# Second attention of a two-layer hybrid block: diagonal chunk mirrored through memory, row sums taken from the output

## The chip, the cores and the metric

The kernel runs on one core of a Trainium2 chip, all data in float32. The metric is device time in microseconds (us) of one launch; lower is better. The profile is of one further execution, recorded by the hardware profiler.

## The reference, cut to what matters

The input `x` is (8, 128, 48, 48): 8 samples, 128 channels, N = 2304 positions. Layer 0 is a group norm and a causal attention with a residual. Layer 1 works on tokens (one per position, 128 channels each):

```
t = tokens of x after layer 0                    # (8, 2304, 128)
h = ln(t)                                        # layer norm over the 128 channels, no gain, no bias
attn = softmax(h @ h^T)                          # "second attention": queries = keys = values = h
t = t + attn @ h
t = t + ffn(ln(t))                               # W, batch norm, then a recurrence over time
```

Two facts of the second attention are used below. The score matrix `h h^T` is symmetric, so the exponential of score (a, b) is also that of (b, a). And since `h` comes out of a layer norm with neither gain nor bias, its 128 channels add up to zero for every token, up to rounding.

## The kernel before, in words

Positions are cut into NB = 18 blocks of P = 128, and into NQ = 6 chunks of QC = 384 (QB = 3 blocks each). For each sample, class `Causal` runs the first attention and class `Full` the second, chunk of queries by chunk of queries. All work items of all samples stand in one list, `stream`; the main loop calls `begin` of item n (score matmul on TensorE, exponential on ScalarE) and `product` of item n - LAG, LAG = 3. So a probability tile is used three items after it was asked for. The first three items of the next sample's causal attention are slipped among the last six items of the second attention.

`Full` has two kinds of item. A **direct** item for key block m computes scores of that block against the 384 queries of chunk j (L1219), exponentiates them into `p` (L1221), and multiplies `p` with the token-major normed block `xhT` into the chunk's PSUM tile `o` (L1233). A direct item whose key chunk n lies behind the query chunk (n > j) is also kept for later: VectorE transposes it in 32 x 32 blocks into tile `t` (L1182), and once the three blocks of a chunk pair are in, `t` is stored to a DRAM tile `e` in one DMA (L1162). When the query chunk is n, the pair is loaded back into `g` by four DMAs, one for each 32 partitions (L1153), which completes the 128 x 128 transposition. A **turned** item then needs a product only (L1229). Chunk j has 3(6 - j) direct items, its own three blocks (the diagonal chunk) among them, and 3j turned ones. Pool `gpool` has three `g` buffers; `prefetch` loads up to three pairs ahead.

Row sums come from three places: ScalarE's accumulator output beside each exponential (`rows`), a VectorE reduction of each full `t` tile (`tsum`, L1190), and a matmul with the 0/1 matrix `same` (L1264) that adds the reduced pieces over partitions, masked by `mine`.

When a chunk is done, `after` copies `o` to SBUF and builds a chain of small steps (`sums`, `residual`, `rooted`, ...). Class `Stream` is a planner: it keeps a clock of its own, `now`, counted in TensorE time, and at every item `tick` emits up to two steps whose due time has come. `advance` and `finish` force steps of a chain out at once. The order of instructions on each engine is the order of emission. Nearly all DMAs are issued by SyncE (SP), in that order; an issue that has to wait holds up those behind it. Scratch tiles of chunk size have one or two buffers (`chunk_tile`), the causal attention's `ta` and `toc` one each. Products' PSUM pool `ps_o` has two buffers, `ps_t` for the chains has two, the pool of `p` six.

The causal attention treats its diagonal chunk by triangles already: item m = 3j + g computes only the columns from g*128 on, and GpSimd (POOL) masks the 128 x 128 block on the diagonal (L1023) before the product. Chain steps of a causal chunk end in `normed` (writes the token-major `xhT`) and `back` (transposes it, writes the channel-major `xh`).

Of the kernel before, what the change touches and what calls it, by code (L numbers as in the profile page):

```python
# [604 lines left out]
def fast_path(ctx: ExitStack, tc: tile.TileContext, x, pe, w_ffn, out, x_tok, w_qkv, w_pos, v_t, gamma_beta, flag):  # L605
    nc = tc.nc
# [60 lines left out]
    with ExitStack() as actx:  # L667
# [93 lines left out]
        for r in range(1 - R, R):  # L761
# [3 lines left out]
        mine = apool.tile([P, NQ - 1, R, QB], F32, tag="mine", name="mine")  # L765
        nc.gpsimd.memset(mine, 1.0)
        nc.gpsimd.affine_select(
            out=mine, in_=mine, compare_op=ALU.is_ge, fill=0.0, base=0, pattern=[[0, NQ - 1], [-SQ, R], [0, QB]], channel_multiplier=1
        )
        nc.gpsimd.affine_select(  # L770
            out=mine, in_=mine, compare_op=ALU.is_ge, fill=0.0, base=SQ - 1, pattern=[[0, NQ - 1], [SQ, R], [0, QB]], channel_multiplier=-1
# [217 lines left out]
        class Causal:  # L989
# [57 lines left out]
            def after(self, j, o):  # L1047
# [25 lines left out]
                def sums():  # L1073

                    tp = psum_t(f"dn_{b}_{j}")
                    k = R * QB
                    nc.tensor.matmul(tp[:, :k], same.rearrange("p a c -> p (a c)"), c["parts"], start=True, stop=True)  # L1077
                    own = small.tile([P, R, QB], F32, tag="ownc", name=f"ownc_{b}_{j}")
                    nc.vector.tensor_mul(own.rearrange("p a g -> p (a g)"), tp[:, :k], mine[:, 0].rearrange("p a g -> p (a g)"))
                    ri = small.tile([P, QB], F32, tag="ric", name=f"ric_{b}_{j}")  # L1080
                    nc.vector.tensor_reduce(ri, own.rearrange("p a g -> p g a"), AX.X, ALU.add)
                    nc.vector.reciprocal(ri, ri)
                    c["ri"] = ri
# [24 lines left out]
                def back():  # L1108
                    tp = transposed(c["y"], f"tb_{b}_{j}")
                    nc.scalar.copy(x_hat[b][1][:, cols], tp[:, :QC])  # L1110

                c["chain"] = normed_chunks[b, j] = st.add([
# [7 lines left out]
                    (back, 0.35, [("ACT", 0.5)]),  # L1120
                ], max(at, st.free["DVE"]) + 0.2 - st.now)

        class Full:
# [6 lines left out]
            def __init__(self, b):  # L1130
                self.b = b
                self.tsum, self.tiles, self.stored, self.loaded = {}, {}, {}, {}
                self.pairs = [(i, j) for j in range(NQ) for i in range(j)]
                self.used, self.to_store = 0, deque()

            @staticmethod
            def items():
                chunks = []
                for j in range(NQ):
                    behind = list(range(j + 1, NQ))  # L1140
                    ahead = [("direct", QB * n + g) for n in ([0] + behind if j == 0 else behind + [j]) for g in range(QB)]
                    turn = [("turned", i, g) for i in range(j) for g in range(QB)]
                    both = [((k + 0.5) / len(ahead), w) for k, w in enumerate(ahead)]
                    both += [((k + 0.5) / len(turn), w) for k, w in enumerate(turn)]
                    chunks.append([w for _, w in sorted(both, key=lambda e: e[0])])
                return listed(chunks)

            def load(self):
                i, j = self.pairs[len(self.loaded)]
                d, _ = self.stored[i, j]  # L1150
                g = gpool.tile([P, R, QB, QB, SQ], F32, tag="g", name=f"g_{self.b}_{i}_{j}")
                for r in range(R):
                    nc.sync.dma_start(  # L1153
                        g[ts(r, SQ)].rearrange("c a j m r -> c a (j m r)"),
                        d.rearrange("(a c) b f -> b c a f", a=R)[r],
                    )
                self.loaded[i, j] = g

            def store(self):
                j, n, t, at = self.to_store.popleft()  # L1160
                d = dpool.tile([P, R, QB * QB * SQ], F32, tag=f"e_{j}_{n}", name=f"e_{self.b}_{j}_{n}")
                nc.sync.dma_start(d, t.rearrange("p b j m r -> p b (j m r)"))  # L1162
                self.stored[j, n] = d, max(at, st.now)

            def prefetch(self):
                while self.to_store and self.to_store[0][3] <= st.now:
                    self.store()
                n = len(self.loaded)
                if n < len(self.pairs) and n < self.used + 3 and self.pairs[n] in self.stored:
                    if self.stored[self.pairs[n]][1] + 6.0 <= st.now:  # L1170
                        self.load()

            def turned(self, j, m, p, ready):
# [12 lines left out]
                if g == QB - 1:  # L1186
                    self.to_store.append((j, n, t, at))
                    if j not in self.tsum:
                        self.tsum[j] = small2.tile([P, NQ - 1, R * QB], F32, tag="tsum", name=f"tsum_{b}_{j}")
                    nc.vector.tensor_reduce(  # L1190
                        self.tsum[j][:, n - j - 1, :], t.rearrange("p b j m r -> p (b j) (m r)"), AX.X, ALU.add
                    )
                    st.then(at, [("DVE", 1.35)])
                    del self.tiles[n]

            def begin(self, j, what, first):
                b = self.b
                if first and j == 0:
                    self.rows = small2.tile([P, NB, NQ], F32, tag="rows", name=f"rows_{b}")
# [9 lines left out]
                if what[0] == "turned":  # L1209
# [5 lines left out]
                    return self.loaded[i, j][:, :, g, :, :].rearrange("p a m r -> p m a r"), 0.0  # L1215
                m = what[1]
                xh = x_hat[b][1]
                s = psum_s(f"s1_{b}_{j}_{m}")
                nc.tensor.matmul(s[:, :QC], xh[:, ts(m, P)], xh[:, ts(j, QC)], start=True, stop=True)  # L1219
                p = pp.tile([P, QC], F32, tag="p", name=f"p1_{b}_{j}_{m}")  # L1220
                nc.scalar.activation(p, s[:, :QC], AF.Exp, bias=shift, accum_out=self.rows[:, m, j : j + 1])  # L1221
                return p, st.then(st.spend(QC * US), [("ACT", 0.58)])

            def product(self, j, what, o, p, ready, first, last):
                xhT = x_hat[self.b][0]
                if what[0] == "turned":
# [3 lines left out]
                    if g == QB - 1:  # L1230
                        self.used += 1
                else:
                    nc.tensor.matmul(o[:, :QC], xhT[:, what[1], :], p, start=first, stop=last)  # L1233
                    st.then(ready, [("ACT", 0.2)])
                    if what[1] // QB > j:
                        self.turned(j, what[1], p, ready)
                st.spend(QC * US, ready)

            def after(self, j, o):
                b, rows, tsum = self.b, self.rows, self.tsum  # L1240
# [4 lines left out]
                if far:  # L1245
                    ot = turn_result(o, f"f_{b}_{j}", c, True)
                    at = st.then(st.now, [("DVE", 0.57)])
                    through = token_major(c, ot, f"f_{b}_{j}", "tof", 4)
                else:
                    o_sb = chunk_tile("o", f"of_{b}_{j}", c, 2)  # L1250
# [5 lines left out]
                def sums():  # L1256

                    dn = small2.tile([P, QB], F32, tag="dn", name=f"dn_{b}_{j}")
                    nc.vector.tensor_reduce(dn, rows[:, QB * j : QB * (j + 1), : j + 1], AX.X, ALU.add)
                    n = NQ - 1 - j  # L1260
                    if n:
                        tp = psum_t(f"ts_{b}_{j}")
                        k = n * R * QB
                        nc.tensor.matmul(  # L1264
                            tp[:, :k], same.rearrange("p a c -> p (a c)"), tsum[j][:, :n, :].rearrange("p n k -> p (n k)"),
                            start=True, stop=True,
                        )
                        own = small2.tile([P, NQ - 1, R, QB], F32, tag="own", name=f"own_{b}_{j}")
                        nc.vector.tensor_mul(
                            own[:, :n].rearrange("p n a g -> p (n a g)"), tp[:, :k], mine[:, :n].rearrange("p n a g -> p (n a g)")  # L1270
                        )
                        more = small2.tile([P, QB], F32, tag="more", name=f"more_{b}_{j}")
                        nc.vector.tensor_reduce(more, own[:, :n].rearrange("p n a g -> p g (n a)"), AX.X, ALU.add)
                        nc.vector.tensor_add(dn, dn, more)
                    ri = small.tile([P, QB], F32, tag="ri", name=f"ri_{b}_{j}")
                    nc.vector.reciprocal(ri, dn)
                    c["ri"] = ri

                def residual():
                    tp = None if far else transposed(o_sb, f"of_t_{b}_{j}")  # L1280
                    t2 = chunk_tile("t2", f"t2_{b}_{j}", c, 5 if last else 2 + F, bufs=1)
# [9 lines left out]
                    if not last:  # L1291
                        c["tt"] = chunk_tile("turn", f"tt_{b}_{j}", c, 5 + F, bufs=1)
# [22 lines left out]
                def fetch():  # L1315
                    c["t2x"] = chunk_tile("t2x", f"t2x_{b}_{j}", c, 7 + F, bufs=1)
                    nc.sync.dma_start(c["t2x"], t2_d[:, b, cols])
                    c["scale"] = chunk_tile("scale", f"scale_{b}_{j}", c, 8 + F, bufs=1)
# [14 lines left out]
                def normed():  # L1333
                    c["x2"] = chunk_tile("t2x", f"x2_{b}_{j}", c, 6, bufs=1)
# [4 lines left out]
                def keep(t2x):  # L1339

                    k = j % (SG // SJ)
                    if before is not None:
                        st.advance(before, 7 if k else len(before.steps) + before.done)
# [14 lines left out]
                def back():  # L1358
                    tp = turned_back(c["x2"], f"tx_{b}_{j}")
                    c["xc"] = chunk_tile("scale", f"xc_{b}_{j}", c, 7, bufs=1)  # L1360
# [21 lines left out]
                else:  # L1382
# [9 lines left out]
                    (sums, 0.15, [("DVE", 0.8)]),  # L1392
                    (residual, 0.0 if far else 0.35, [("DVE", 3.2)]),
# [243 lines left out]
```

## Time and profile before

| what | value |
|---|---|
| median of 3 runs | 1771.99 us (1771.1 to 1772.96) |
| profiled execution, its own time | 1769.93 us |
| its span, first to last instruction | 1768.1 us |
| mean granted TensorE clock | 0.993 |
| busy: PE / DVE / ACT / POOL | 1739.9 / 1299.7 / 762.5 / 194.9 us |
| instructions | 22177 |
| moved by DMA | 262.00 MB |

PE is TensorE's matmuls, PEld its weight loads (they overlap), DVE is VectorE, ACT is ScalarE, POOL is GpSimd, SP is SyncE. A float32 matmul shows as two PE records, so 504 matmuls read x1008. A PE record's duration runs from its start to its end and overlaps the next record's: the price of a matmul is the distance between starts, not the mean in the row. From one sample's start to the next the profile repeats every 207.65 us (a sample's same three-product group starts at 645.10 and at 852.76 us); a last stage of some 65 us is the recurrence.

### The profile page before, as it was taken

How to read it: one execution, taken by the hardware profiler on the slowest of the kernel's cores; microseconds unless marked ns; L12 is line 12 of the kernel's file. 1: busy time of each engine (PE TensorE's matmuls, PEld its weight loads, DVE VectorE, ACT ScalarE, POOL GpSimd, SP SyncE). 2: the span in 40 equal slices, each digit the busy share in tenths (PEclk: the TensorE clock that was granted, in tenths of full speed). 3: DMA queues.
4: the chain of work that ended last, by engine and by line, in shares of the span. 5: the costliest groups of instructions: out<-in, count | busy, mean ns of one | idle time of the engine just before them, and what ended most of it. 6: DMA issues, size and time to landing. Idle time of an engine off the chain costs nothing.

```text
span 1768.1 us, 22177 instructions
## 1 busy us (share of the span) xinstructions
PE 1739.9 (98%) x6215; PEld 1092.2 (62%) x6215; DVE 1299.7 (74%) x3355; ACT 762.5 (43%) x1836; POOL 194.9 (11%) x301
## 2 busy tenths in 40 slices
PE   9999999999999999999999999999999999999996
PEld 5666566665666566665666656665666656666565
DVE  4868668876887668786687767876687866877467
ACT  2344434443345434444344443454344543444445
POOL 1110011100110001100111001200011001110006
PEclk8999999999999999999999999999999999999998
DMA  3405672257533584156731575334832468116768
GB/s 141 139 23 182 184 203 93 89 184 193 146 103 121 157 235 130 47 167 183 209 99 68 190 197 157 107 108 157 228 120 77 148 183 217 56 46 199 194 231 217
DMA packets 206056, 262.00 MB, mean 148 GB/s; under 512 B 90113, under 2 KB 175010, under 8 KB 205412
## 3 DMA queue, kind: packets, MB, share of 16 engines
q1 hardware_dynamic: 204972, 257.47, 48.2%
q0 software_dynamic: 720, 2.62, 1.0%
q8 instruction: 52, 0.85, 0.2%
q14 instruction: 80, 0.66, 0.1%
q10 hardware_dynamic: 232, 0.40, 0.1%
HBM read 150.24 MB, written 110.17 MB: 147 GB/s over the span
## 4 chain that ended last, share of the span: by engine, by line
PE 96%; DMA 1%; DVE 1%; ACT 1%; issue 0%; SPq 0%; POOL 0%; ACTq 0%; DVEq 0%; POOLq 0%
PE o L1233 19%; PE s L1219 19%; PE s L1018 17%; PE o L1029 17%; PE o L1229 13%; PE pj L879 4%; PE pj L882 2%; PE z L1550 2%; PE wx L1325 2%; PE of_t L939 1%; PE tb L939 1%; PE pb L837 0%; DMA x<-in_x_dram 0%; PE dn L1077 0%; PE ts L1264 0%
## 5 line engine op out<-in xcount | busy, mean ns | idle before, releaser
L1221 ACT ACTIVATE p<-s,shift 128x384 f32<-128x384 f32 x504 | 292.3, 580 | 479.1 <-PE s L1219 464.5
L1020 ACT ACTIVATE p<-s 128x384 f32<-128x384 f32 (+2 forms) x504 | 231.6, 460 | 426.0 <-PE s L1018 372.1
L1219 PE MATMUL s<-xh 128*128 128x384 f32 x1008 | 410.6, 489 | 0.0
L1233 PE MATMUL o<-p,xhT 128*128 128x384 f32 x1008 | 404.2, 488 | 5.8 <-ACT p L1221 5.8
L1018 PE MATMUL s<-q,k 128*128 128x384 f32 (+2 forms) x1008 | 382.1, 461 | 0.1
L1029 PE MATMUL o<-p,vT 128*128 128x384 f32 (+2 forms) x1008 | 377.6, 457 | 0.0
L1229 PE MATMUL o<-g,xhT 128*128 128x384 f32 x720 | 281.3, 489 | 0.5 <-issue 0.5
L1233 PEld LDWEIGHTS o<-p,xhT 128*128 128x128 f32 x1008 | 189.4, 190 | 133.2 <-ACT p L1221 10.3
L1029 PEld LDWEIGHTS o<-p,vT 128*128 128x128 f32 x1008 | 189.2, 191 | 114.3 <-issue 0.6
L1219 PEld LDWEIGHTS s<-xh 128*128 128x128 f32 x1008 | 186.7, 191 | 114.8
L1018 PEld LDWEIGHTS s<-q,k 128*128 128x128 f32 x1008 | 183.2, 191 | 96.9 <-issue 0.9
L1044 DVE TENSOR_TENSOR acc<-acc,p 128x384 f32<-128x384 f32 (+2 forms) x408 | 208.9, 512 | 33.0 <-POOL p L1023 8.7
L1182 DVE STREAM_TRANSPOSE t<-p 128x384 f32<-128x384 f32 x360 | 187.2, 550 | 37.6 <-ACT p L1221 35.9
L1229 PEld LDWEIGHTS o<-g,xhT 128*128 128x128 f32 x720 | 133.6, 191 | 82.5 <-DMA g<-e 0.7
L1190 DVE TENSOR_REDUCE tsum<-t 128x12 f32<-128x1152 f32 x120 | 162.4, 1353 | 4.2
L884 DVE TENSOR_TENSOR z<-pj,pb 128x384 f32<-128x384 f32 x144 | 78.9, 548 | 109.3 <-PE pj L879 92.7
L1023 POOL TENSOR_TENSOR p<-p,triu 128x128 f32<-128x128 f32 x144 | 72.5, 505 | 607.4 <-ACT p L1020 476.5
L1299 POOL TENSOR_TENSOR roots<-ve_f,mhalf 128x3 f32<-128x3 f32 x48 | 40.8, 849 | 520.6 <-DVE ve_f L923 520.6
L1221 ACT ACTIVATION_READ_ACCUMULATOR p<-s,shift 128x1 f32 x504 | 97.2, 193 | 0.0
L879 PE MATMUL pj<-xn,wT 128*128 128x384 f32 x192 | 79.9, 501 | 1.4 <-DVE xn L872 1.4
L929 POOL TENSOR_TENSOR rs_c<-ve_c,mhalf 128x3 f32<-128x3 f32 x48 | 45.4, 947 | 215.6 <-DVE ve_c L923 215.6
L1326 DVE TENSOR_TENSOR scale<-wx,scale 128x384 f32<-128x384 f32 x46 | 25.4, 552 | 55.6 <-PE wx L1325 50.6
(242 smaller groups left out, 1471.0 us busy)
## 6 DMA issues: line engine op xcount, KB each, us to landing
e<-t SPq DMA_DIRECT2D x120, 576.0 KB
g<-e SPq DMA_DIRECT2D x480, 144.0 KB
pb<-posb_d SPq DMA_DIRECT2D x46, 576.0 KB
t1t<-in_x_tok_dram SPq DMA_DIRECT2D x48, 192.0 KB
t_d<-tt SPq DMA_DIRECT2D x184, 48.0 KB
t2x<-t_d SPq DMA_DIRECT2D x46, 192.0 KB
scale<-rs SPq DMA_DIRECT2D x46, 192.0 KB
x<-in_x_dram SPq DMA_DIRECT2D x14, 576.0 KB
```

Source lines behind the costliest of these rows:

```text
L879: nc.tensor.matmul(ps[:, :QC], wT[:, j, :], xn, start=True, stop=True)
L884: nc.vector.tensor_add(z, ps[:, :QC], c["pb"][:, j, :])
L1018: nc.tensor.matmul(s[:, off:QC], keys[b][:, ts(m, P)], queries[b, j][:, off:], start=True, stop=True)
L1020: nc.scalar.activation(p[:, off:], s[:, off:QC], AF.Exp, scale=SCALE)
L1029: nc.tensor.matmul(o[:, off:QC], vals[b][:, ts(m, P)], p[:, off:], start=first, stop=last)
L1044: nc.vector.tensor_add(a[:, off:], a[:, off:], p[:, off:])
L1182: nc.vector.transpose(t[:, :, :, g, :].rearrange("p b j r -> p j b r"), p.rearrange("p (j b r) -> p j b r", j=QB, b=R))
L1190: nc.vector.tensor_reduce(self.tsum[j][:, n - j - 1, :], t.rearrange("p b j m r -> p (b j) (m r)"), AX.X, ALU.add)
L1219: nc.tensor.matmul(s[:, :QC], xh[:, ts(m, P)], xh[:, ts(j, QC)], start=True, stop=True)
L1221: nc.scalar.activation(p, s[:, :QC], AF.Exp, bias=shift, accum_out=self.rows[:, m, j : j + 1])
L1229: nc.tensor.matmul(out_ap, xhT[:, QB * i + g, :], p, start=first, stop=last)
L1233: nc.tensor.matmul(o[:, :QC], xhT[:, what[1], :], p, start=first, stop=last)
```

## The change

1. **Mirror.** A direct item of the diagonal chunk (m = 3j + g) computes only the columns from g*128 on, for the score, the exponential and the product. The products left out come from transposes: blocks right of the diagonal of items g = 0 and g = 1 are transposed by VectorE in 32 x 32 blocks into `tm` (the tag of the causal `ta`), written to DRAM in one DMA, and read back by four DMAs into `gm` (the tag of the causal `to`). Two **mirrored** items per chunk, g = 1 (128 columns) and g = 2 (256 columns), stand at the end of the chunk and need a product only. The item g = 0 of the diagonal chunk is put first in the chunk, and the diagonal items come ahead of the other direct ones.
2. **Row sums.** The accumulator output, `rows`, `tsum`, the matmul with `same` and the step `sums` go. A new last step of each causal chain, `shifted`, adds 1 to `xhT` and takes 1 off the residual `t1_tok`, both on POOL. Each output row then holds the attention result plus the row sum in every channel; `residual` gets the row sum as the mean over the 128 channels of the transposed result, and the surplus of 1 after division is cancelled by the lowered residual.
3. **Turned tiles.** The four-piece split moves from the load to the store: `t` is stored by four DMAs, and `g` is loaded whole by one.
4. The counts of chain steps are adapted (one step fewer ahead of `residual`).

```diff
     chain of a causal chunk:
+                def shifted():
+                    nc.gpsimd.tensor_scalar_add(c["y"], c["y"], 1.0)
+                    nc.gpsimd.tensor_scalar_add(t1_tok[b, j], t1_tok[b, j], -1.0)
                     (back, 0.35, [("ACT", 0.5)]),
+                    (shifted, 0.0, [("POOL", 1.2)]),
     Full.items:
-                    ahead = [("direct", QB * n + g) for n in ([0] + behind if j == 0 else behind + [j]) for g in range(QB)]
+                    ahead = [("direct", QB * n + g) for n in range(j, NQ) for g in range(QB)]
...
+                    order_of.insert(0, order_of.pop(first))
+                chunks.append(order_of + [("mirrored", g) for g in range(1, QB)])
     Full.load, Full.store:
-                for r in range(R):
-                    nc.sync.dma_start(
-                        g[ts(r, SQ)].rearrange("c a j m r -> c a (j m r)"),
-                        d.rearrange("(a c) b f -> b c a f", a=R)[r],
-                    )
+                nc.sync.dma_start(g.rearrange("p a j m r -> p (a j m r)"), d.rearrange("p a f -> p (a f)"))
-                nc.sync.dma_start(d, t.rearrange("p b j m r -> p b (j m r)"))
+                turned = d.rearrange("(b c) a f -> a c b f", b=R)
+                for r in range(R):
+                    nc.sync.dma_start(turned[r], t[ts(r, SQ)].rearrange("c b j m r -> c b (j m r)"))
+            def mirror(self, j, g, p, ready):
+                b, left = self.b, QB - 1 - g
+                if g == 0:
+                    if j == 0:
+                        st.advance(normed_chunks[b, NQ - 1], 1)
+                    self.tm = chunk_tile("ta", f"tm_{b}_{j}", bufs=1).rearrange("p (b q r) -> p b q r", b=R, q=QB)
+                first = g * (QB - 1)
+                nc.vector.transpose(
+                    self.tm[:, :, first : first + left, :].rearrange("p b q r -> p q b r"),
+                    p[:, (g + 1) * P :].rearrange("p (q b r) -> p q b r", q=left, b=R),
+                )
...
+                gm = chunk_tile("toc", f"gm_{b}_{j}", {}, bufs=1).rearrange("p (a q r) -> p a q r", a=R, q=QB)
...
+                def out_of():
+                    nc.sync.dma_start(d, tm.rearrange("p b q r -> p b (q r)"))
+                def back_in():
+                    for r in range(R):
+                        nc.sync.dma_start(
+                            gm[ts(r, SQ)].rearrange("c a q r -> c a (q r)"), d.rearrange("(a c) b f -> b c a f", a=R)[r]
+                        )
+                self.moved = st.add([(out_of, 0.0, [("", 5.0)]), (back_in, 0.0, [("", 5.0)])], at + 0.2 - st.now)
     Full.turned, last block of a pair:
-                    nc.vector.tensor_reduce(
-                        self.tsum[j][:, n - j - 1, :], t.rearrange("p b j m r -> p (b j) (m r)"), AX.X, ALU.add
-                    )
     Full.begin:
+                if what[0] == "mirrored":
+                    st.finish(self.moved)
+                    return self.gm.rearrange("p a q r -> p q a r"), 0.0
-                nc.tensor.matmul(s[:, :QC], xh[:, ts(m, P)], xh[:, ts(j, QC)], start=True, stop=True)
+                nc.tensor.matmul(s[:, off:QC], xh[:, ts(m, P)], xh[:, j * QC + off : (j + 1) * QC], start=True, stop=True)
-                nc.scalar.activation(p, s[:, :QC], AF.Exp, bias=shift, accum_out=self.rows[:, m, j : j + 1])
+                nc.scalar.activation(p[:, off:], s[:, off:QC], AF.Exp, bias=shift)
     Full.product:
+                elif what[0] == "mirrored":
+                    g = what[1]
+                    cols = g * P
+                    out_ap = o[:, :cols].rearrange("p (m a r) -> p m a r", m=g, a=R)
+                    nc.tensor.matmul(out_ap, xhT[:, QB * j + g, :], p[:, g - 1 : 2 * g - 1], start=first, stop=last)
     Full.after, the step sums goes; in residual, after the transposes of the result:
+                    nc.vector.tensor_reduce(dn, by_token, AX.XY if far else AX.X, ALU.add)
+                    nc.vector.tensor_scalar_mul(dn, dn, 1.0 / P)
+                    ri = c["ri"] = small.tile([P, QB], F32, tag="ri", name=f"ri_{b}_{j}")
+                    nc.vector.reciprocal(ri, dn)
```

## The prediction, on record before the changed kernel ran

> **What bounds the kernel now.** I read the busy totals and the slices first, then the chain that ended last, then the groups of instructions, then the windows and the timeline of single stages.
>
> ```profile
> PE 1739.9 (98%) x6215; PEld 1092.2 (62%) x6215; DVE 1299.7 (74%) x3355; ACT 762.5 (43%) x1836; POOL 194.9 (11%) x301
> PE   9999999999999999999999999999999999999996
> PE 96%; DMA 1%; DVE 1%; ACT 1%; issue 0%; SPq 0%; POOL 0%; ACTq 0%; DVEq 0%; POOLq 0%
> ```
>
> PE is at nine tenths or more in all slices but the last, and 96% of the chain that ended last is PE. A busy PE need not be a PE at its peak, so I check that it has no holes and what a matmul really takes. Windows inside the samples (columns: length, then PE, PEld, DVE, ACT, POOL busy, clock, DMA share, GB/s):
>
> ```profile
> 220.00:330.00 110.00, 110.00 (x406) 70.07 (x405) 84.91 (x244) 43.77 (x89) 15.13 (x25) 1.00 0.46 133
> 540.00:640.00 100.00, 99.38 (x335) 59.94 (x335) 73.31 (x175) 45.50 (x124) 4.80 (x6) 1.00 0.58 178
> ```
>
> The first is causal, the second is second attention: PE has no gap in the one and 0.6 us in the other. No other engine or the DMA is near its limit. Prices from the timeline (start, duration, then the instruction):
>
> ```profile
> 657.13 0.59 PE L1018 MATMUL s<-q,k 128*128 128x256 f32 x2
> 657.56 0.81 PE L1229 MATMUL o<-g,xhT 128*128 128x384 f32 x2
> 658.21 0.81 PE L1219 MATMUL s<-xh 128*128 128x384 f32 x2
> ...
> 659.49 0.39 PE L1018 MATMUL s<-q,k 128*128 128x128 f32 x2
> 659.72 0.81 PE L1229 MATMUL o<-g,xhT 128*128 128x384 f32 x2
> ```
>
> Distances between starts: 256 columns 0.43 us, 384 columns 0.65, 128 columns 0.23. Time follows the columns; narrow matmuls pay no visible surcharge for their weight load. The turned product L1229, which reads a strided tile as the mirrored one will, costs the same 0.65.
>
> **What the Trainium skill says.** "Perfetto Trace Analysis", Identifying the Most-Contended Engine, warns that matmul occupancy is not closeness to the roofline. The trace agrees: the row of L1219 says 489 ns a record, the starts say 323. "DMA: Bandwidth & Descriptors", Anatomy of one DMA, puts a fixed part of about 2 us on each DMA, most of it the receipt of the write; here a 192 KB load took 4.26 us and a store of `t2c` 2.86 us on the chain that ended last. "GPSIMD Engine Reference", Engine selection, calls POOL about two times slower than VectorE for two inputs and near line rate for one; POOL's two-input 128x128 takes 455 ns in the trace, its one-input select of that size 303.
>
> **The change, part by part.**
>
> *Scores of the diagonal chunk (PE).* Three scores of 384 columns (1.94 us) become 384 + 256 + 128 (0.65 + 0.43 + 0.23 = 1.31). The products lose the same columns, but the mirrored items bring them back: 1.31 + 0.43 + 0.23 = 1.97 against 1.94. Net 0.60 us a chunk; 48 chunks: **-28.8 us**, on the path.
>
> *Matmul of the row sums (PE).* 40 of them (chunks 0 to 4), gone:
>
> ```profile
> 650.10 0.81 PE L879 MATMUL pj<-xn,wT 128*128 128x384 f32 x2
> 650.74 0.29 PE L1264 MATMUL ts<-tsum,same 128*128 128x12 f32 x2
> 650.88 0.89 PE L1229 MATMUL o<-g,xhT 128*128 128x384 f32 x2
> 651.61 0.81 PE L879 MATMUL pj<-xn,wT 128*128 128x384 f32 x2
> ```
>
> From 650.74 to 651.61 are 0.87 us for this one and a product of 0.65: 0.22 us each, **-9.0 us**.
>
> *VectorE and ScalarE.*
>
> ```profile
> L1182 DVE STREAM_TRANSPOSE t<-p 128x384 f32<-128x384 f32 x360 | 187.2, 550 | 37.6 <-ACT p L1221 35.9
> L1190 DVE TENSOR_REDUCE tsum<-t 128x12 f32<-128x1152 f32 x120 | 162.4, 1353 | 4.2
> L1221 ACT ACTIVATION_READ_ACCUMULATOR p<-s,shift 128x1 f32 x504 | 97.2, 193 | 0.0
> ```
>
> 162 us leave VectorE with L1190, some 37 us with the small operations of `sums`; 48 mirror transposes of 256 and of 128 columns (by the 550 ns row 0.38 + 0.20, 28 us) and 48 channel sums with scaling and reciprocal (a 384-wide reduction takes 0.55 in L1071; 0.55 + 0.17 + 0.17, 43 us) come: net -128. ScalarE loses 97 us and some exponential columns. Both are covered by PE: **0**, except at the very end, where no PE work follows and the channel sum lies in the chain: +0.9 us. If the cover goes (VectorE late in chunk 0, where the causal chain of chunk 5 meets the mirror transposes), `p` stays taken, and the exponential is late next; I allow 0 to 8 x 0.5 us.
>
> *POOL.* 48 times two one-input operations of 384 columns. No row shows one; bounds: the 512-wide two-input row is 1.84 us, so under 1.4; the 128-wide select above 0.3. I take 0.7 each, 67 us in all, cover: POOL is busy 11%. Queued behind them is the triangle mask of the causal diagonal (L1023). In the timeline the mask of the first diagonal block ends at 657.13 and its product starts at 658.85: 1.7 us of slack. A collision costs up to 1.4 + 0.45 - 1.7, seldom: **0**, bound +6.
>
> *Turned tiles.* Issues on SP stay 5 a pair. An issue takes 0.43 us for a quarter tile, 0.34 to 0.38 for a whole one. A load becomes one issue instead of 1.8 us, a store four; loads are the urgent ones, so this helps where chunk 5 consumes a tile every 2 us. Stores hold `t` some 1.5 us longer; two `t` buffers, one tile per 3.9 us: VectorE may lag, PE not: **0**, bounds -2 to +3. In chunk 4 the pair (4, 5) is now stored near the chunk's end; by PE time I count 12 us until its product, against 10 for store, planned gap and load.
>
> *The mirror's way through memory.* This is the new wait: the transposes on VectorE, one store of 192 KB, four loads of 48 KB (384-byte pieces) that SP issues only after the store has landed, then the product. Queued behind that SP wait are `g` loads and the chain's DMAs; behind the product stands all of PE. SP gets 48 x (0.38 + 4 x 0.43) = 101 us of issues more, 6% of the span. Round trip by the DMAs above: store 2.9 to 4.3, issues 1.7, landing of the last 2.9 to 4.3: **7.5 to 10.3 us**. Time that PE has until it needs `gm`: in chunks 0 to 4 the item g = 1 is at place 1 to 4 of 20, so 12 us and more: nothing. In chunk 5 it is at place 8. Adding the PE work of the loop from its product to the mirrored one (turned 0.65, three causal items of the next sample, chain steps left out) gives 9.9 us, and `p` is ready about 1 us earlier. So it mostly just fits: I take 0.5 us for seven samples. In the last sample no causal items follow: 6.2 + 1 us of time, a wait of 2.5. Sum **+6**, bounds 0 and +24 (3 us in each of the 8).
>
> *Two small ones.* At the end of chunk 5 the next causal product needs the PSUM buffer that ScalarE still copies; exponential and copy take 1.2 us, the last mirrored product and one score 1.07: +0.3 x 7 = **+2**. `residual`, now the first step, can meet a copy of `o` not yet done (L1251): **+1**.
>
> Sum: -28.8 - 9.0 + 0.9 + 6 + 2 + 1 = **-27.9, say -29**, as the freer SP should shorten the last tail (at 1682 a `t2x` load waits behind `g` issues on the chain) by about 1. Against the profiled execution, 1769.93, that is 1741; the median of the runs is 2.1 us higher: 1743.
>
> **The rivals.**
>
> *All waits hidden* (0.3): PE had no holes in 110 us windows though dozens of round trips ran beside it; then only the removals and the tail stay, -37: 1735.
>
> *Mirror late in chunk 5 only* (0.14): SP holds other waits (the queue's own waits show up to 25 us on L1162), so the store or the loads start late. 2 to 4 us in each of 8 samples beyond my sum, -5 to -20: 1752 to 1767.
>
> *Slower* (0.08): mirrored products at the chunk's end wait everywhere. It decides once the wait exceeds 37.8 / 48 = 0.79 us per chunk; since chunks 0 to 4 have 12 us and more, it needs round trips of over 13 us, or 4.7 us per sample in chunk 5 alone, a trip of over 15. With SP blocked on a store whose tile is not ready this can happen; 1.5 us a chunk would give 1772 + 34 = 1806. Against it: the causal result takes the same path (store, four loads), and SP waited for that store 24.3 us in 18 waits, 4.8 at most.
>
> *The change does not do what it says*: a 128-column matmul might cost as much as a wide one. The prices above exclude it.
>
> **How the numbers follow.** Main case 0.45, around 1743, own range 1737 to 1750; all hidden 0.3; chunk 5 late 0.14; slower 0.08; the rest, no change to speak of, 0.03. A measurement can tell about 0.2% from no change, 3.5 us. Faster 0.88, same 0.04, slower 0.08. The range leaves out the slower case and half of chunk 5 late: 1731 (all removals, -2 for the loads, tail -2) to 1758.
>
> **What would show it right or wrong.** Right: two score rows of 256 and 128 columns at 48 each, no `ts` row, PE still nine tenths in all slices, a repeat of about 203.5 us per sample instead of 207.65, PE's wait for `gm` under 10 us in total and in chunk 5 only. Wrong: a releaser DMA on the `gm` products of many chunks, waits of `p` L1023 on POOL that reach PE, or an unchanged repeat.

## The result: slower, 1814 us, and where TensorE now waits

The changed kernel takes 1814.37 us (median of 4 runs), the kernel before 1772.47 us beside it: ratio 1.024, 95% interval 1.0224 to 1.0256. The profiled execution took 1813.87 us, its span 1812.2, its mean granted TensorE clock 0.976 (before 0.993). The prediction was 1743, range 1731 to 1758. Of all executions below, one of e12 ran in a slower state of the chip (2042.91 us, clock 0.827); it is in e12's median and not in its ratio.

The page of the changed kernel: busy totals, PE's slices, the chain that ended last.

```profile
PE 1725.7 (95%) x6326; PEld 1105.1 (61%) x6327; DVE 1188.3 (66%) x3259; ACT 699.5 (39%) x1332; POOL 319.0 (18%) x397
PE   9999899998999989998999989999899989999886
PE 84%; DMA 7%; SPq 4%; issue 2%; DVE 2%; ACT 1%; POOL 0%; DVEq 0%; POOLq 0%; ACTq 0%
```

PE has an eight in about one slice per sample, where it had nines (an eight is 80 to 90% busy). In the chain it falls from 96% to 84%; DMA and SP's queue, 1% and 0% before, carry 11%. Groups of the changed kernel (busy, mean of one | idle before it, releaser):

```profile
L1223 DVE STREAM_TRANSPOSE t<-p 128x384 f32<-128x384 f32 x360 | 184.1, 550 | 107.0 <-DMA e<-t 68.0
L1274 PE MATMUL o<-gm,xhT 128*128 128x128 f32 x192 | 51.5, 370 | 59.1 <-DMA gm<-m 59.1
L1114 POOL TENSOR_SCALAR xhT<-xhT 128x384 f32<-128x384 f32 x48 | 60.0, 1251 | 186.5 <-PE tb L939 186.5
```

The mirrored product (L1274) stands idle 59.1 us for `gm`. No other PE row has an idle time like that, and the wait for `g` is small. The repeat per sample is now 212.2 us (the product after the long wait starts at 637.99 and at 850.18), against 207.65. Inside one repeat, 850.18 to 1062.37, PE is busy 204.60 us: 7.6 us are holes.

The timeline around one long wait, at the end of chunk 3 of a sample (start, duration, engine, instruction; SP rows are the issues of DMAs):

```profile
829.04 0.60 PE L1278 MATMUL o<-p,xhT 128*128 128x256 f32 x2
829.24 0.56 DVE L1308 TENSOR_REDUCE dn<-of_t 128x3 f32<-128x384 f32 x1 [2.45 <-PE of_t L939]
...
833.03 0.27 DVE L1191 STREAM_TRANSPOSE tm<-p 128x128 f32<-128x128 f32 x1
833.33 0.34 SPq L1204 DMA_DIRECT2D m<-tm  x1
835.40 0.39 SPq L1386 DMA_DIRECT2D out_dram<-t2c  x1
835.84 2.67 SPq L1387 DMA_DIRECT2D t2l_d<-t2c  x1
838.60 1.57 SPq L1341 DMA_DIRECT2D rs<-roots_t  x3
840.21 1.86 SPq L1344 DMA_DIRECT2D t_d<-tt  x4
842.17 1.82 SPq L1172 DMA_DIRECT2D e<-t  x4
844.10 0.39 SPq L1164 DMA_DIRECT2D g<-e  x1
844.52 2.05 SPq L1208 DMA_DIRECT2D gm<-m  x4
...
850.18 1.62 PE L1274 MATMUL o<-gm,xhT 128*128 128x128 f32 x4 [6.13 <-DMA gm<-m]
851.59 1.49 PE L1278 MATMUL o<-p,xhT 128*128 128x384 f32 x2
852.87 1.37 PE L879 MATMUL pj<-xn,wT 128*128 128x384 f32 x2
```

The product of the diagonal item g = 1 starts at 829.04. VectorE gets to its transpose only at 833.03, behind the chain step `residual`, whose first operation, the channel sum, sat 2.45 us waiting for TensorE's transposes. SP issues the mirror's store at 833.33. Then the queue is taken: first SP waits for `t2c`, and of the 9.1 us from 835.40 to 844.49 it issues for 8.7. The loads of `gm`, planned 5 us after the store, leave 11.2 us after it; the last lands 3.6 us after the end of its issue, as PE restarts at 850.18. From store to landing: 16.8 us; from the product of item g = 1: 21 us.

The windows of that stretch show two more things (length, PE, PEld, DVE, ACT, POOL busy, clock, DMA share, GB/s):

```profile
844.00:850.00 6.00, 0.05 (x1) 0.00 (x0) 0.45 (x1) 0.09 (x1) 0.00 (x0) 0.76 1.01 273
850.00:854.00 4.00, 3.82 (x8) 2.50 (x9) 0.00 (x0) 0.48 (x1) 0.00 (x0) 0.50 0.92 265
```

While PE waits, the 16 DMA engines are full: `gm` lands among a store and a load of 576 KB each, issued just ahead of it. And after the hole TensorE runs at half clock for 4 us: a 384-column product takes 1.28 us from start to start instead of 0.65, which costs about 2 us more (an estimate: half of 4 us).

### The profile page after: what moved, and what is told of

Same layout as the page of the kernel before. It is cut to its first block, busy times and chain, and to the rows that moved or that the text cites. A ratio compares the mean times of both kernels' runs of the same rounds, so it can differ in the third digit from the quotient of the medians.

```text
span 1812.2 us, 22179 instructions
## 1 busy us (share of the span) xinstructions
PE 1725.7 (95%) x6326; PEld 1105.1 (61%) x6327; DVE 1188.3 (66%) x3259; ACT 699.5 (39%) x1332; POOL 319.0 (18%) x397
## 4 chain that ended last, share of the span: by engine, by line
PE 84%; DMA 7%; SPq 4%; issue 2%; DVE 2%; ACT 1%; POOL 0%; DVEq 0%; POOLq 0%; ACTq 0%
PE s L1018 16%; PE o L1029 16%; PE s L1256 15%; PE o L1278 15%; PE o L1266 9%; DMA g<-e 3%; PE pj L879 3%; DMA gm<-m 2%; PE o L1274 2%; PE z L1580 2%; PE pj L882 1%; PE wx L1356 1%; SPq L1208 1%; PE tb L939 1%; PE of_t L939 1%
## 5 line engine op out<-in xcount | busy, mean ns | idle before, releaser
L1258 ACT ACTIVATE p<-s,shift 128x384 f32<-128x384 f32 (+2 forms) x504 | 274.8, 551 | 550.9 <-PE s L1256 466.7
L1256 PE MATMUL s<-xh 128*128 128x384 f32 (+2 forms) x1008 | 379.5, 458 | 0.0
L1278 PE MATMUL o<-p,xhT 128*128 128x384 f32 (+2 forms) x1008 | 376.5, 462 | 1.8 <-ACT p L1258 1.8
L1023 POOL TENSOR_TENSOR p<-p,triu 128x128 f32<-128x128 f32 x144 | 79.0, 554 | 557.6 <-ACT p L1020 556.7
L1274 PE MATMUL o<-gm,xhT 128*128 128x128 f32 x192 | 51.5, 370 | 59.1 <-DMA gm<-m 59.1
L1114 POOL TENSOR_SCALAR xhT<-xhT 128x384 f32<-128x384 f32 x48 | 60.0, 1251 | 186.5 <-PE tb L939 186.5
L1274 PEld LDWEIGHTS o<-gm,xhT 128*128 128x128 f32 x192 | 35.0, 212 | 78.2 <-DMA gm<-m 53.5
L1191 DVE STREAM_TRANSPOSE tm<-p 128x256 f32<-128x256 f32 x96 | 34.1, 361 | 55.9 <-ACT p L1258 55.0
```

Source lines behind the costliest of these rows:

```text
L1023: nc.gpsimd.tensor_mul(p[:, off : off + P], p[:, off : off + P], triu)
L1256: nc.tensor.matmul(s[:, off:QC], xh[:, ts(m, P)], xh[:, j * QC + off : (j + 1) * QC], start=True, stop=True)
L1258: nc.scalar.activation(p[:, off:], s[:, off:QC], AF.Exp, bias=shift)
L1274: nc.tensor.matmul(out_ap, xhT[:, QB * j + g, :], p[:, g - 1 : 2 * g - 1], start=first, stop=last)
L1278: nc.tensor.matmul(o[:, off:QC], xhT[:, what[1], :], p[:, off:], start=first, stop=last)
```

## Experiments

The leading theory, A: TensorE waits for `gm`, whose trip is late on SP's queue and on the DMA engines. Rivals: B, the new row sums (POOL work, the channel sum); C, the four-piece stores. The kernel before measured 1769.6, 1772.05 and 1770.35 us beside e1 to e4, e5 to e8 and e9 to e12.

**e1, the mirror undone.**

```diff
-                return max(0, m - QB * j) * P if m < QB * (j + 1) else 0
+                return 0
-                chunks.append(order_of + [("mirrored", g) for g in range(1, QB)])
+                chunks.append(order_of)
-                    elif g < QB - 1:
-                        self.mirror(j, g, p, ready)
```

> Undoes the mirror alone: the diagonal chunk is again computed in full width (three scores and three products of 384 columns), no transposes into tm, no trip through memory. Row sums from the raised result, the split at the store and the new order of items stay. Theory A (PE waits for the mirrored tiles gm, whose trip is late on SP's queue): the 74 us of stalls go and the 28.8 us of saved scores come back; what stays is the missing row-sum matmul, so about 1764 us. Rival B (the row sums: the two POOL operations and the channel sum that stalls VectorE): still 1795 or more. Rival C (four-piece stores that hold t and SP): still 1795 or more.

Measured 1764.95 us, ratio 0.997 (0.9961 to 0.9979). This is theory A's figure. The slowdown is gone with the mirror, and B and C fall as its cause: their work is all still there.

**e2, the trip left out.**

```diff
-                self.moved = st.add([(out_of, 0.0, [("", 5.0)]), (back_in, 0.0, [("", 5.0)])], at + 0.2 - st.now)
+                self.gm = tm.rearrange("p a q r -> p a q r")
-                    st.finish(self.moved)
```

> Leaves out the trip through memory only: the mirrored products read tm, the tile that VectorE wrote, so the 32 x 32 blocks are not brought to their partitions and the products of the mirrored blocks use the wrong values. TensorE's, VectorE's, ScalarE's and POOL's work is that of the changed kernel. Theory A: no wait for gm, the repeat per sample falls from 212.3 to about 203, so 1738 us. Rivals B and C: 1790 or more, as their causes are all still there.

Measured 1731.17 us, ratio 0.9771 (0.9751 to 0.9791). Busy totals of e2:

```profile
PE 1703.2 (98%) x6326; PEld 1097.7 (63%) x6327; DVE 1188.8 (69%) x3259; ACT 698.7 (40%) x1332; POOL 309.3 (18%) x397
```

All operations of the changed kernel on TensorE, VectorE, ScalarE and POOL are there, and it is 38.4 us faster than the kernel before, 7 us more than theory A asked for: TensorE's saving is real, and the row sums on POOL and VectorE cost nothing that shows. The trip alone costs 83 us (1814 less 1731).

The two traces also say how TensorE loses them. In the changed kernel it waits 59.1 us for `gm`. And PE is busy 1725.7 us, here 1703.2, for the same 6326 records: 22.5 us more, an estimate of what the half clock after the holes costs in all. The two make 81.6 of the 83 us.

**e3, pieces at the load again.** The two functions `load` and `store` as before the change.

> Undoes only where the pieces are: t is stored whole by one DMA and g loaded by four, as before the change; mirror and row sums stay. Theory A: SP issues as many DMAs, but the 1.8 us of e stores that stand ahead of the gm loads turn into 0.4, and g loads take more; the wait for gm shrinks a little, 1800 to 1815 us. Rival C: the loss was the stores, so 1745 or less. Rival B: 1814.

Measured 1841.66 us, ratio 1.0399 (1.0381 to 1.0417): 27 us more, outside all three forecasts. The wait for `gm` grew (total us, times, longest):

```profile
PE o L1276 <- DMA gm<-m: 71.6, 16, 5.6
```

So part 3 of the change helps where the mirror is. With four pieces on the loading side, `g` and `gm` together need eight issues of SP where five are needed now; that this is the whole reason was not tried.

**e4, the way back planned earlier.**

```diff
-                self.moved = st.add([(out_of, 0.0, [("", 5.0)]), (back_in, 0.0, [("", 5.0)])], at + 0.2 - st.now)
+                self.moved = st.add([(out_of, 0.0, [("", 1.5)]), (back_in, 0.0, [("", 5.0)])], at + 0.2 - st.now)
```

> The planned gap between the mirror's store and its loads is 1.5 us instead of 5.0, so the four gm loads stand earlier in SP's order, ahead of most of the chain's DMAs; nothing else changes. Theory A in the form that SP's order makes the trip late: the wait in chunk 3 (6 us) mostly goes, the one in chunk 4 partly, 1755 to 1790 us. Theory A in the form that the DMA engines are full and gm lands late whatever the order: 1805 to 1815. Rivals B and C: 1814.

Measured 1784.91 us, ratio 1.0073 (1.0052 to 1.0094), in the range of the theory that SP's order makes the trip late. 29 us come back by order alone. But of the 61.5 us that PE waited for `gm` and `g` (59.1 and 2.4) more than half is still there, at another tile:

```profile
PE o L1266 <- DMA g<-e: 36.9, 23, 4.1
```

No wait for `gm` is left. With the loads of `gm` early in its order, SP stands longer at the landing of the mirror's store (128.7 us in all, 52.3 in the changed kernel), and the next `g` loads are late. The wait has moved from the mirrored to the turned product.

**e5 and e6, another issuing engine.** `nc.sync` becomes `nc.scalar` or `nc.gpsimd` in `out_of` and `back_in`.

> The mirror's store and four loads are issued by ScalarE instead of SP; bytes, pieces and plan stay. If the trip is late because it stands in SP's queue (issues of 0.4 us each in order, held by other waits), the wait for gm nearly goes: 1735 to 1755 us, less what ScalarE loses by issuing 5 DMAs a chunk (2 us of 44) and by waiting for tm and for the store. If the trip is late because the 16 DMA engines are full, the wait stays: 1795 or more.

Measured 1804.71 us, ratio 1.0184 (1.0153 to 1.0215).

> The same five DMAs issued by POOL. Late by SP's queue: 1735 to 1760 us, as POOL is nearly idle in the second attention; late by full DMA engines: 1795 or more. Should POOL take much longer for one issue than SP, the trip may be late again, 1760 to 1790, with the wait for gm named in the trace.

Measured 1787.95 us, ratio 1.0102 (1.0085 to 1.0119). Waits of e5 and then of e6:

```profile
PE o L1266 <- DMA g<-e: 35.4, 19, 5.9
PE o L1274 <- DMA gm<-m: 12.1, 13, 1.6
```

```profile
PE o L1274 <- DMA gm<-m: 23.9, 7, 3.6
PE o L1266 <- DMA g<-e: 14.7, 11, 4.0
```

Both times lie outside the range that was given for a trip late by SP's queue alone. e5 has the time of the other range, 1795 or more, but not its reason: the wait for `gm` fell from 59.1 to 12.1 us, and the wait for `g` came up. e6 falls in its third range, with the wait for `gm` named; one issue took 0.55 us on POOL (median) against 0.43 on SP. Leaving SP's queue gives 10 and 26 us, not 60: TensorE still waits for both tiles, and in e5 ScalarE's exponentials, which follow the issues on the same engine, wait too (51 us put down to `gm`). So SP's order is not the only resource short here.

**e7, the mirror by TensorE.**

```diff
-                nc.vector.transpose(
...
+                tp = psum_t(f"mt_{b}_{j}_{g}")
+                for q in range(left):
+                    nc.tensor.transpose(tp[:, ts(q, P)], p[:, ts(g + 1 + q, P)], ident)
+                nc.scalar.copy(self.tm[:, ds(first * P, left * P)], tp[:, : left * P])
```

> The mirrored blocks are made by TensorE: three 128 x 128 transposes a chunk into PSUM and a ScalarE copy into tm, no VectorE transposes and no trip through memory; all else as in the changed kernel. Theory A: no wait for gm; TensorE pays 0.33 us a chunk (three transposes, by the row of of_t) on top of the run without the trip, 1731 + 16 = 1747 us. Rivals B and C were refuted by the first runs for the bulk of the loss; if something of theirs is left in the second attention it shows as more than 1755.

Measured 1753.23 us, ratio 0.9904 (0.9886 to 0.9922): faster than both kernels, 6 us above the sum of 1747. The trace shows 6.7 us of waits for `g` in it.

**e8, the trip made, but not waited for.**

```diff
-                    return self.gm.rearrange("p a q r -> p q a r"), 0.0
+                    return self.tm.rearrange("p a q r -> p q a r"), 0.0
```

> The trip through memory is made as in the changed kernel, by the same DMAs on SP, but the mirrored products read tm, so nobody waits for gm (the blocks are not brought to their partitions, the mirrored values are wrong). If the loss is TensorE's wait for gm alone: 1731 to 1740 us as without the trip. If the trip costs by what it does to SP's queue and the DMA engines (g loads, chain DMAs late): 1750 to 1790.

Measured 1778.9 us, ratio 1.0047 (1.0028 to 1.0066). Nobody waits for `gm`, and still it is 48 us slower than e2. The busy totals and a wait of e8 say how:

```profile
PE 1721.2 (97%) x6326; PEld 1102.8 (62%) x6327; DVE 1190.1 (67%) x3259; ACT 699.7 (39%) x1332; POOL 318.3 (18%) x397
```

```profile
PE o L1266 <- DMA g<-e: 37.5, 17, 6.3
```

The trip makes the turned tiles late: TensorE waits 37.5 us for `g`, and PE is busy 18.0 us longer than in e2. This was the surprise, and it corrects theory A. The trip loads the path that `g` shares, and TensorE then stands at whichever tile it needs first: at `gm` in the changed kernel, where the wait for `g` is 2.4 us, at `g` where nobody needs `gm`. So 48 us are what the trip costs when it is not waited for, and taking the wait for `gm` away brings 35 of the 83; they are not two parts that stand side by side in the changed kernel's trace.

**e9, the issues without the bytes, and e10, the bytes with fewer issues.** Both start from e8; only added lines are shown.

```diff
e9:
+                    nc.sync.dma_start(d[:4], tm[:4].rearrange("p b q r -> p b (q r)"))
+                            gm[r * SQ : r * SQ + 1].rearrange("c a q r -> c a (q r)"), d[r : r + 1]
e10:
+                    nc.sync.dma_start(gm.rearrange("p a q r -> p (a q r)"), d.rearrange("p a f -> p (a f)"))
```

> As e8 (mirrored products read tm, nobody waits for gm), but the five DMAs of the trip move next to nothing: the store takes 4 of the 128 partitions, each load one partition. SP issues the same five DMAs with the same waits. If SP's issue time and its waits for tm and for the store make g late: 1765 to 1780, like e8's 1779. If the bytes and pieces on the 16 DMA engines do: 1731 to 1745, like the run without the trip.

> As e8, but the way back is one whole load (128 rows of 1536 bytes) instead of four loads in pieces of 384 bytes: the same bytes, two issues on SP instead of five, a quarter of the pieces; the waits stay. If the four issues and their small pieces make g late: 1740 to 1755. If it is the bytes, or SP's waits for tm and the store: 1770 to 1780.

Measured 1752.81 us (ratio 0.9894, 0.9877 to 0.9912) and 1753.91 us (0.9904, 0.9887 to 0.992). Waits of e9 and then of e10:

```profile
PE o L1266 <- DMA g<-e: 23.9, 16, 4.3
```

```profile
PE o L1263 <- DMA g<-e: 23.1, 15, 4.6
```

e9 lies between its two forecasts, e10 in its first. Either lightened trip costs some 22 us over e2, the full one of e8 48. They are not two halves: e10 keeps two of the five issues and the waits. Five near-empty DMAs on SP with their waits are enough to make `g` late; taking away the bytes, or three of the four load issues and their 384-byte pieces, brings 25. How much of the rest is issue time and how much SP's standing at a wait was not separated, nor was the part, if any, of the two buffers that `tm` and `gm` share with the causal chain.

**e11 and e12, the trip in chunks 0 to 2 alone.** In chunks 3 to 5, e11 computes the diagonal chunk in full, e12 mirrors by TensorE as e7 does.

```diff
e12:
+                        (self.mirror if j < 3 else self.flipped)(j, g, p, ready)
```

> The mirror is kept in chunks 0 to 2 alone; in chunks 3 to 5 the diagonal chunk is computed in full. If the trips hurt only where the g loads are dense (chunks 3 to 5): TensorE keeps half of the saved scores, 14.4 us, and the 9 us of the row sums, 1749 us, with no wait for gm or g in the trace. If a trip costs the same in every chunk: half of e8's 48 us stays, 1770 or more.

Measured 1757.56 us, ratio 0.9929 (0.9912 to 0.9945). PE waits neither for `gm` nor for `g`, as forecast, so it is the place of the trip that decides; but 13 us were won, not 21. The trace shows 9.9 us of waits of causal products for ScalarE and 4.0 of scores for `xh`, waits that e2 has not; why they come was not tried.

> Chunks 0 to 2 mirror through memory as in the changed kernel, chunks 3 to 5 by TensorE: three 128 x 128 transposes into PSUM and a ScalarE copy. By the run without the trip (1731) plus 24 times 0.33 us of transposes: 1739 to 1746 us, faster than both kernels and than the mirror by TensorE in all chunks (1753). If the trips of the early chunks cost anything, 1750 or more.

Measured 1742.09 us, ratio 0.9826 (0.9806 to 0.9845): as forecast, and the fastest version that does the whole computation, ahead of both kernels and of e7. PE's waits for `g` total 3.7 us in it.

## Why the prediction was wrong, point by point

*Scores and row-sum matmul, -37.8.* Right: with the 0.9 for the longer tail -36.9 was forecast; e2, which holds all parts but the trip, gave -38.4, and PE's busy time fell by 36.7 in it (1739.9 to 1703.2). Forty times 0.22 us are 8.8, not 9.0. The rows are there: 96 records each of the scores of 256 and 128 columns, and no `ts`.

*VectorE, ScalarE, POOL at 0.* Right as to cost (e2), wrong as to size on POOL: one operation takes 1.25 us (L1114), not 0.7. VectorE's one-input operation of that width takes 0.47 (L872, kernel before), so the "near line rate" that the prediction took from the Trainium skill ("GPSIMD Engine Reference", Engine selection) is not what this trace shows. VectorE lost 111 us of work, not 128.

*Turned tiles, bounds -2 to +3.* The mechanism named, that stores hold `t` and VectorE lags, is in the trace (68 us of waits for `e<-t`), and in e2, with 57.3 us of them, PE waits for nothing of it. The benefit was undersized: with the mirror in place, loading whole is worth the 27 us of e3.

*The mirror's way through memory, +6, bounds 0 to +24: the step that failed.* It measured +83: 59.1 us of waits for `gm` and 22.5 us of slower work after them. Three terms of it were wrong.

1. "In chunks 0 to 4 ... 12 us and more: nothing." The time PE gave was sized right: 15 us from 829.04 to its stop at 844.05. The trip was not 7.5 to 10.3 but 16.8 from the store, and 21 from the product. The estimate added the landing times of DMAs and their own issues. It left out what SP issues between the store and the loads, which stand 11.2 us apart in chunk 3, and VectorE's 4 us before the store. The prediction itself counted "101 us of issues more, 6% of the span" and charged them nothing; a mean share says nothing on a queue that is full for 9 us on end. Most of the delay came before the last load was issued at all; with the engines full, its landing then took 3.6 us.
2. The wait was looked for in chunk 5. It came at the ends of chunks 3 and 4 (6.1 and 1.6 us in the sample shown), where SP carries chain DMAs, `e` stores and `g` loads at once. In chunk 5 of that sample PE has none.
3. "Queued behind that SP wait are `g` loads" was written, and not priced. In the changed kernel this is hidden behind the wait for `gm`; e8 shows it uncovered, 48 us.

*The rivals.* The slower rival named the mechanism, late mirrored products at the chunk's end with SP blocked, but wanted them late in all chunks, or in chunk 5 alone, and had 0.08. In fact two chunks of six sufficed, with 6 us in one of them. The argument against it, that the causal result takes the same store and loads with 24.3 us of SP's waits in all, was no evidence: in the trace before, TensorE waits 0.2 us in all for what VectorE makes of those loads. They have time to spare; `gm` had not. The rival of a late chunk 5 was summed wrongly: 2 to 4 us in each of 8 samples on top of -29 give -13 to +3, not -5 to -20; with the right sum, too, 1814 lies far outside it.

*The two small terms, +2 and +1.* Nothing of that size shows: in e2 TensorE waits for ScalarE's copy of `o` once, 0.6 us.

*The half clock* had no place in the sum at all, and it is about a quarter of the loss. It belongs to any forecast in which a gap of some us opens on TensorE.

## What to carry to other kernels

When a tile that the bounding engine needs is sent through memory, price the trip by its queue: list, in order, what the issuing engine has to issue and wait for between the store and the load, and what traffic the load lands in; then ask what its waits hold up behind it. A DMA path that is busy half of the time on average (0.53 in the repeat of the changed kernel) can be full where it matters (1.01 in the window above). A trip added there was paid even when nobody waited for it (e8). Three transposes by TensorE, 0.33 us a chunk, were cheaper than the free ones by VectorE that need memory; and the trip was free of waits only in the chunks where the other loads were few (e11, e12).

## What the runs showed of the hardware

After a hole of 6.1 us TensorE ran at half its clock for about 4 us (window above). The Trainium skill, "TensorE: Matmul & The Clock Gate", HAM oscillation, speaks of idle gaps beyond about 3.4 us. The eight long holes of the changed kernel, 4.5 to 6.6 us, agree, each with spacings of 1.28 us after it; e8 shows the same after a shorter one. Its windows, a hole and what follows:

```profile
841.00:843.50 2.50, 0.00 (x0) 0.00 (x0) 1.97 (x5) 0.03 (x1) 0.00 (x0) 1.00 0.97 357
843.50:848.50 5.00, 4.97 (x10) 2.79 (x11) 0.58 (x1) 0.58 (x1) 0.00 (x0) 0.66 0.56 224
```

So a wait of 2.6 us already brought a slow stretch, while one of 1.6 us, at 873.66 in the changed kernel, was followed by a 384-column spacing of 0.65 us. The runs give no single limit in between: in e8 a wait of 2.07 us (ended at 1263.69) was followed by spacings of 1.28 us, one of 2.73 us (428.78) by 0.65 at once, and so was one of 2.94 us in e4 (427.91). What else decides stays open.

A one-input POOL operation on 128 x 384 float32 took 1.25 us in place and 1.18 us on the residual, 2.7 times the 0.455 us (median, kernel before) of a two-input operation of a third of the width: a column costs about the same with one input as with two.
